# Self products of eight batches moved to the load of adj, with the schedule's ranks set anew, in a two-layer graph network on one core

## The chip, the cores and the metric

One core of one Trainium2 chip runs the whole program. The metric is device time in microseconds, the median of several runs. TensorE is PE in the profile, VectorE is DVE, ScalarE is ACT, GpSimd is POOL and SyncE is SP. SP only issues DMAs here.

## The reference, cut to what matters

Sixteen batches `x` of 1024 nodes by 128 features share one 0/1 matrix `adj`. Layer 0 is a graph attention, layer 1 a gated update that is repeated five times; each layer ends in a residual and a norm.

```python
# layer 0
h   = x @ others_weight
att = softmax(where(adj > 0, leaky_relu(u1[idx1] + u2[idx2]), -9e15), axis=1)
x   = layernorm(x + att @ h + x @ self_weight)
# layer 1, five steps: av = [adj @ h, adj @ h]
u3  = h @ u3_w.T
z   = sigmoid(av @ w3_w.T + u3);  r = sigmoid(av @ w4_w.T + u3)
hv  = tanh(av @ w5_w.T + (r * h) @ u5_w.T)
h   = (1 - z) * h + z * hv
out = layernorm(x + h)
```

(The biases are left out here.) The change is about `x + x @ self_weight`, which the kernel makes as one product of `x` with `self_w + identity`.

## The kernel before, in words

Everything lies transposed, features on the 128 partitions and nodes along the free side, in two halves of 512. `adj` stays in SBUF as `adj`, and four sums of its quarters as `tab`.

**Layer 0** (`layer0(b)`, for each batch b). The batch is loaded into a tile `xt` (two buffers). Eight small products `ps_g_ph` (L602) make `h`, which ACT copies to `hx`. Softmax weights follow on DVE and ACT. Scaled blocks `blk` (each as a high and a low part, by `hi_` on ACT and `lo_` on DVE) are multiplied with `adj` into `ps_acc_po` (L573). The self product x times `wsi` (`self_w` plus identity) is made by two matmuls for each batch: L858 into its own PSUM bank `ps_acc_px` for the left half, which DVE adds at L865, and L872 at the start of the accumulation of `ps_acc_po` for the right half, whose sum ACT copies out at L884. Then come a transpose, the norm (`layernorm`: DVE statistics, POOL power, ACT scale) and a transpose back into the state `hT`.

**Layer 1** works on pairs of batches (q = b // 2). `messages(q, s, k)` multiplies the states of a pair with `adj` in step s, by a scheme with seven products from `adj` and `tab` (banks `ps_acc_a`, `gz`, `ps_acc_c`), or plainly (`ps_acc`) for the (pair, step) in `PLAIN`. `gates(b, s, soon)` then does for each half: L1103 (u3 times h), ACT copy to `gz`, L1113 twice (gates r and z), tanh on ACT, r times h on DVE, L1129 and L1130 (candidate), tanh on ACT, three DVE operations that update `hT`. `leave(b, s)` turns the new state for the next step: a 32x32 transpose on DVE (L531), four DMAs to DRAM (`away`), one back (`back`, tile `G`), and a split into high and low parts (L561 on ACT, L565 on DVE). For the (pair, step) in `TURNED` it uses four TensorE transposes (L523) instead. After the last step `o` tiles (two buffers) take the first layer's result from DRAM (L1197), DVE adds (L1205), a norm follows, and L1216 stores the output.

**The order of the work** is not that of the code. Each operation is given to `Plan` with an engine, a length, a rank and what it reads and writes. `Plan.order()` plays these through on an own clock: an engine that is free takes the ready operation with the lowest rank whose buffers can be had. The program is emitted in that order, and each engine runs its list strictly in that order. DVE and ACT lengths are multiplied by `MARGIN`. The dictionary `D` holds rank offsets by kind of operation; `rank_of(b, s)` is 10 for each pair and 4.2 for each step, with `LATER` added for the last batch.

**Fillers.** `IDLE` operations of rank 9000, of two transposes of the identity each (L413), fill the places where, by the plan's clock, TensorE has nothing ready. All of them write one PSUM tile `("ps", "idle")`; it is one of the six buffers of kind `ps`, and by the plan it is held from the first filler to the last. `gz` has two more buffers.

The parts below are those that the change touches.

Of the kernel before, what the change touches and what calls it, by code (L numbers as in the profile page):

```python
# [9 lines left out]
F32 = mybir.dt.float32  # L10
# [3 lines left out]
ALU = mybir.AluOpType  # L14
AX = mybir.AxisListType

P = 128
N = 1024
HALF = 512
NC = N // P  # L20
STEPS = 5
# [4 lines left out]
LOW, HIGH = -20.0, 100.0  # L26
TINY = 1e-30
PLAIN = {(0, 0), (0, 1), (0, 2), (7, 2), (7, 3), (7, 4)}
LATER = 3
TURNED = {(7, 3)}  # L30
IDLE = 100


class Plan:
# [4 lines left out]

    MARGIN = 1.15
    SAME = {"PE": 0, "DVE": 60, "ACT": 60, "POOL": 60, "SP": 2500, "DMA": 0}
    LAG = {"PE": 250, "DVE": 150, "ACT": 170, "POOL": 200, "SP": 2500, "DMA": 2400}

# [87 lines left out]
def kernel(  # L133
# [51 lines left out]
    nc = tc.nc  # L185
    B = x_t.shape[0]
# [6 lines left out]
    wsi = const.tile([P, P], F32, tag="wsi", name="wsi")  # L193
# [19 lines left out]
    def exact(pools):  # L213

        def pool(name, bufs, space=None):
# [35 lines left out]
            "D": (6, [P, HALF], F32, bass.MemoryType.DRAM),  # L251
            "X": (24, [P, HALF + 16], F32, bass.MemoryType.DRAM),
            "yd": (24, [P, HALF], F32, bass.MemoryType.DRAM),
            "ud": (2, [3, N], F32, bass.MemoryType.DRAM),
            "ps": (6, [P, HALF], F32, PS),
            "gz": (2, [P, HALF], F32, PS),
# [39 lines left out]

        D = dict(m=-0.4, pu=1.4, u=0.4, pr=0.8, pz=1.4, r=-0.3, pv=0.2, z=0.3, hv=0.2, h=0.6, tr=1.0, o=3.6, ln=3.9)
        D.update(out=4.2, l1=-9, l2=-5, l3=-4, l4=-4, l5=-5, l6=-3.5, l7=-1, l8=0)

        def on_pe(b, what):  # L300

# [9 lines left out]
        def rank0(b):  # L311
            return 10 * (b // 2) - 1 * (1 - b % 2) + -1.0
# [6 lines left out]
        boot = ("hT", "boot")  # L319
# [99 lines left out]
        for k in range(kinds["gz"][0]):  # L419
            pe(F, -99, lambda k=k: fill_(k), reads=[(("ident",), 0)], writes=[(("gz", "fill", k), 0)])  # L420

        for i in range(IDLE):
            pe(2 * TR, 9000, idle_, reads=[(("ident",), 0)], writes=[(("ps", "idle"), 0)])

# [3 lines left out]
        def sums():  # L428
# [5 lines left out]
            nc.vector.tensor_tensor(bh, bias[:, 0:2], bias[:, 3:4].to_broadcast([P, 2]), ALU.add)  # L434
            nc.vector.tensor_scalar(bh, bh, 0.5, None, ALU.mult)

        def own_weights():
            pb_ = ("ps", "g", "b")
            pe(150, -4.6, lambda: column_(pb_, slice(2 * P, 3 * P), 5), reads=[(ws, "b"), (("rz", 0), 1)], writes=[(pb_, 0)])
            dve(160, -4.3, lambda: nc.vector.tensor_copy(bias, T(pb_)[:, 0:5]), reads=[(pb_, 0)], writes=[(("bias",), 0)])  # L440
            dve(270, -4.5, self_, reads=[(boot, "ws"), (("ident",), 0), (("zs", 0), NC - 1)], writes=[(("wsi",), 0)])
            dve(1000, -4.2, sums, reads=[(boot, "late"), (("bias",), 0), (("uw",), 0), (("rz", 0), 1)], writes=[(("wm",), 0)])

        def adj_tables(c):
# [16 lines left out]
        def quarter(i, j):  # L461
            return lambda c: adj[:, 4 * i + c, j * HALF : (j + 1) * HALF]
# [107 lines left out]
        def product(bank, blk, right, first, last, cs=range(4), seeded=False):  # L570
            terms = [(k, c) for c in cs for k in range(2)]
            for i, (k, c) in enumerate(terms):
                nc.tensor.matmul(  # L573
                    T(bank),
                    T(blk)[:, k, c, :],
                    right(c),
                    start=(first and i == 0),
                    stop=(last and i == len(terms) - 1),
                    skip_group_check=seeded,
                )  # L580


        def layer0(b):
# [266 lines left out]
            def add_():  # L850
                nc.vector.tensor_tensor(T(yT[0]), T(yT[0]), T(yT[1]), ALU.add)

            dve(V, rank, add_, reads=[(yT[0], "p"), (yT[1], "p")], writes=[(yT[0], "s")])
            px = ("ps", "acc", b, "px")
            pe(
                F,
                rank,
                lambda: nc.tensor.matmul(T(px), wsi, T(xt)[:, left], start=True, stop=True),  # L858
                reads=[(xt, 0), (("wsi",), 0), (yT[1], "p")],
                writes=[(px, 0)],  # L860
            )
            dve(
                V,
                rank,
                lambda: nc.vector.tensor_tensor(T(yT[0]), T(px), T(yT[0]), ALU.add),  # L865
                reads=[(px, 0), (yT[0], "s")],
                writes=[(yT[0], 0)],
            )
# [3 lines left out]
                nc.tensor.matmul(T(po2), wsi, T(xt)[:, right], start=True, stop=False)  # L872

            begun = [(hl[1][0], c, 1) for c in range(4)]
            pe(F, rank, px2_, reads=[(xt, 1), (("wsi",), 0), *begun], writes=[(po2, 0)])
            for g in range(2):
                pe(
                    8 * R,
                    rank,
                    lambda g=g: product(po2, hl[1][g], quarter(g, 1), False, g == 1),  # L880
                    reads=[(k, 4 * g + c, j) for k, j in ((hl[1][g], 0), (hl[1][g], 1), (("A",), 1)) for c in range(4)],
                    writes=[(po2, 0)],
                )
            act(A, rank, lambda: nc.scalar.copy(T(yT[1]), T(po2)), reads=[(po2, 0), (yT[0], "s")], writes=[(yT[1], 0)])  # L884

            for g in range(2):
                rank = rank0(b) + D["l5"]
# [271 lines left out]
        def leave(b, s):  # L1159

            rank = rank_of(b, s)
            hT = ("hT", b)
            for g in range(2):

                def h(g=g):
                    return T(hT)[:, g * HALF : (g + 1) * HALF]

                k, d = ("T", b, s, g), ("X", b, s + 1, g)
                if s < STEPS - 1 and on_pe(b, s):
                    t = ("ps", "t", b, s, g)  # L1170
# [23 lines left out]
                sp(  # L1194
                    450,
                    rank + D["o"],
                    lambda o=o, yd=yd: nc.sync.dma_start(T(o).rearrange("p c d -> p (c d)"), T(yd)),  # L1197
                    reads=[(yd, 0), (hT, g)],
                    writes=[(o, "y")],
                )  # L1200

                def last(t=t, o=o, flat=on_pe(b, s)):
                    x = T(o).rearrange("p c (a j) -> p c a j", a=4)
                    n = T(t).rearrange("p (c a j) -> p c a j", c=4, a=4) if flat else chunks(T(t))
                    nc.vector.tensor_tensor(x, n, x, ALU.add)  # L1205
# [55 lines left out]
        def sum_flags():  # L1261
            nc.tensor.matmul(T(("ps", "t", "flag"))[0:1, 0:2], T(("rstd", "ends"))[:, 0, 3:4], ones, start=True, stop=True)

        for c in range(NC):
            adj_tables(c)
        for c in range(NC // 2):
# [4 lines left out]
        for k, (q, s) in enumerate(sorted(pairs, key=lambda x: rank_of(2 * x[0], x[1]))):  # L1271
            soon = messages(q, s, k)
            for b in (2 * q, 2 * q + 1):
                gates(b, s, soon)
                leave(b, s)
        for i in range(2 * NC):
            look_at(i)
        late = rank_of(B, 0) - 2
# [280 lines left out]
```

## Time and profile before

| what | value |
|---|---|
| median of 3 runs | 1466.42 us (1464.65 to 1471.49) |
| profiled execution | 1466.58 us, of which the span is 1464.7 us |
| granted TensorE clock, mean | 0.994 |
| PE busy | 1442.1 us (98%), 5052 matmul records |
| DVE busy | 1168.4 us (80%) |
| ACT busy | 898.9 us (61%) |
| POOL busy | 152.9 us (10%) |
| DMA | 174.21 MB, 119 GB/s over the span |
| fillers L413 | 200 matmul records, 4.9 to 49.4 us |
| L858 and L872, the self products | 16 matmuls each (32 records each) |

A 128x512 product of full fp32 shows as two records, a product with `adj` (in `float32r`) and a 128x128 transpose as one. Records of neighbouring matmuls overlap in time, so what one costs is read from start to start, not from its duration. Busy time counts the overlap once. "Idle before" is the time for which an engine stood still ahead of an instruction, with what released it.

### The profile page before, as it was taken

The page shows a single profiled execution, that of the slowest core. Times are in us where ns is not written, and L with a number is a line of the kernel's source. Part 1 is how long each engine was busy: PE and PEld are TensorE (multiplying, and loading weights), DVE is VectorE, ACT ScalarE, POOL GpSimd, SP SyncE. Part 2 cuts the span into 40 slices and gives each one's busy share as a digit, 9 for nine tenths or more (in the row PEclk, how much of TensorE's full clock was granted, in tenths as well). Part 3 has the DMA queues.
Part 4 walks back from the last instruction along what each step waited for, and adds up shares of the span by engine and source line. Part 5 has one row for each costly group of instructions (what it writes and reads, how often), then busy time and mean ns, then how long its engine had stood idle before and what let it go on. Part 6 is the DMA issues. An engine that isn't in the chain of part 4 may idle for free.

```text
span 1464.7 us, 17943 instructions
## 1 busy us (share of the span) xinstructions
PE 1442.1 (98%) x5052; PEld 904.6 (62%) x5052; DVE 1168.4 (80%) x2757; ACT 898.9 (61%) x1792; POOL 152.9 (10%) x265
## 2 busy tenths in 40 slices
PE   9999899999999999999999999999999999999995
PEld 7766665666666666665566656665666665665563
DVE  6887788888888788888888888887888877757444
ACT  5456565676657666576756676566674666555544
POOL 0201000011002020110201120011110202000102
PEclk9999999999999999999999999999999999999998
DMA  4145534654335542464433643355433464223301
GB/s 164 58 126 162 167 78 117 172 177 128 87 100 151 173 131 65 121 172 140 117 98 117 187 123 94 108 161 155 116 85 96 134 184 114 58 72 87 91 24 45
DMA packets 208384, 174.21 MB, mean 119 GB/s; under 512 B 34879, under 2 KB 158486, under 8 KB 208278
## 3 DMA queue, kind: packets, MB, share of 16 engines
q1 hardware_dynamic: 207714, 172.15, 41.1%
q10 hardware_dynamic: 564, 0.85, 0.2%
q8 instruction: 41, 0.67, 0.2%
q14 instruction: 65, 0.53, 0.1%
HBM read 94.63 MB, written 78.29 MB: 118 GB/s over the span
## 4 chain that ended last, share of the span: by engine, by line
PE 94%; DVE 2%; DMA 1%; ACT 1%; POOL 1%; issue 0%; SPq 0%; POOLq 0%; DVEq 0%
PE ps_acc_a L573 17%; PE ps_g_r L1113 9%; PE ps_g_v L1129 9%; PE ps_g_v L1130 9%; PE gz L1113 9%; PE ps_g_r L1103 9%; PE ps_acc_c L573 8%; PE ps_acc_po L573 8%; PE ps_acc L573 6%; PE gz L573 4%; PE ps_g_ph L602 2%; PE ps_idle L413 1%; PE ps_acc_po L872 1%; PE ps_acc_px L858 1%; ACT o L510 1%; DMA blk_boot<-in_adj_dram 0%
## 5 line engine op out<-in xcount | busy, mean ns | idle before, releaser
L1129 PE MATMUL ps_g_v<-m,wm 128*128 128x512 f32 x320 | 163.4, 592 | 0.0
L1130 PE MATMUL ps_g_v<-r,u5h 128*128 128x512 f32 x320 | 163.3, 592 | 0.0
L1140 DVE TENSOR_TENSOR hv<-hv,hT 128x512 f32<-128x512 f32 x160 | 109.7, 687 | 63.2 <-ACT hv L1133 62.8
L1113 PE MATMUL ps_g_r<-m,wm 128*128 128x512 f32 x320 | 158.8, 594 | 1.1 <-ACT gz L1106 1.1
L1113 PE MATMUL gz<-m,wm 128*128 128x512 f32 x320 | 157.7, 592 | 0.0
L1103 PE MATMUL ps_g_r<-hT,u 128*128 128x512 f32 x320 | 152.7, 592 | 0.0
L1123 DVE SCALAR_TENSOR_TENSOR r<-r,hT 128x512 f32<-128x512 f32 x160 | 109.1, 686 | 50.9 <-ACT r L1116 50.1
L573 PE MATMUL ps_acc_a<-tab,blk_s 128*128 128x512 f32 x544 | 146.7, 411 | 0.4 <-ACT m L1056 0.4
L573 PE MATMUL ps_acc_po<-adj,blk 128*128 128x512 f32 x512 | 144.5, 428 | 0.0
L1116 ACT ACTIVATE r<-ps_g_r,bh 128x512 f32<-128x512 f32 x160 | 109.4, 686 | 46.8 <-PE ps_g_r L1113 46.5
L573 PEld LDWEIGHTS ps_acc_a<-tab,blk_s 128*128 128x128 f32 x544 | 100.4, 188 | 34.4 <-issue 6.7
L1116 ACT ACTIVATE z<-gz,bh 128x512 f32<-128x512 f32 x160 | 109.5, 688 | 19.1 <-PE gz L1113 18.8
L573 PEld LDWEIGHTS ps_acc_po<-adj,blk 128*128 128x128 f32 x512 | 96.0, 188 | 39.4 <-issue 14.6
L1154 DVE SCALAR_TENSOR_TENSOR hT<-hv,hT 128x512 f32<-128x512 f32 x160 | 107.9, 676 | 1.6
L1147 DVE SCALAR_TENSOR_TENSOR hv<-z,hv 128x512 f32<-128x512 f32 x160 | 108.1, 677 | 1.0 <-ACT z L1116 0.3
L1106 ACT COPY gz<-ps_g_r 128x512 f32<-128x512 f32 x160 | 91.5, 574 | 28.1 <-PE ps_g_r L1103 26.7
L531 DVE STREAM_TRANSPOSE T<-hT 128x512 f32<-128x512 f32 x150 | 104.9, 701 | 4.1 <-DMA X<-T 3.7
L1130 PEld LDWEIGHTS ps_g_v<-r,u5h 128*128 128x128 f32 x320 | 60.5, 189 | 76.8 <-issue 61.9
L1113 PEld LDWEIGHTS gz<-m,wm 128*128 128x128 f32 x320 | 60.5, 190 | 74.4 <-issue 74.0
L573 PE MATMUL ps_acc<-adj,blk_h 128*128 128x512 f32 x384 | 99.9, 416 | 3.9 <-DVE blk_h L565 3.9
L1133 ACT ACTIVATE hv<-ps_g_v,nb 128x512 f32<-128x512 f32 x80 | 54.9, 689 | 68.6 <-PE ps_g_v L1130 68.6
L1113 PEld LDWEIGHTS ps_g_r<-m,wm 128*128 128x128 f32 x320 | 59.4, 189 | 58.5 <-issue 44.6
(166 smaller groups left out, 2520.7 us busy)
## 6 DMA issues: line engine op xcount, KB each, us to landing
G<-X SPq DMA_DIRECT2D x152, 256.0 KB
X<-T SPq DMA_DIRECT2D x600, 64.0 KB
yd<-y SPq DMA_DIRECT2D x32, 256.0 KB
o<-yd SPq DMA_DIRECT2D x32, 256.0 KB
out_dram<-o SPq DMA_DIRECT2D x32, 256.0 KB
xt<-in_x_dram SPq DMA_DIRECT2D x15, 512.0 KB
pb<-ud SPq DMA_DIRECT2D x14, 512.0 KB
D_y<-T_y SPq DMA_DIRECT2D x112, 64.0 KB
```

What stands on the lines that cost most here:

```text
L531: nc.vector.transpose(T(t).rearrange("p (b c i) -> p b c i", b=4, c=4), turned(src()))
L573: nc.tensor.matmul(T(bank), T(blk)[:, k, c, :], right(c), start=(first and i == 0), stop=(last and i == len(terms) - 1), skip_group_check= ...
L1103: nc.tensor.matmul(T(pr), u3, h(), start=True, stop=True)
L1106: nc.scalar.copy(T(pz), T(pr))
L1113: nc.tensor.matmul(T(p_), wm[:, j, :], T(m), start=False, stop=True, skip_group_check=True)
L1116: nc.scalar.activation(T(t), T(p_), AF.Tanh, bias=bh[:, j : j + 1], scale=0.5 * sg)
L1123: lambda r=r, h=h: nc.vector.scalar_tensor_tensor(T(r), T(r), 1.0, h(), ALU.add, ALU.mult),
L1129: nc.tensor.matmul(T(pv), wm[:, 2, :], T(m), start=True, stop=False)
L1130: nc.tensor.matmul(T(pv), u5h, T(r), start=False, stop=True)
L1140: lambda hv=hv, h=h: nc.vector.tensor_tensor(T(hv), T(hv), h(), ALU.subtract),
L1147: lambda hv=hv, z=z: nc.vector.scalar_tensor_tensor(T(hv), T(z), 1.0, T(hv), ALU.add, ALU.mult),
L1154: lambda hv=hv, h=h: nc.vector.scalar_tensor_tensor(h(), T(hv), 0.5, h(), ALU.mult, ALU.add),
```

## The change

The self product of batches 4 to 11 (`AHEAD`) is made at the start of the program. Each of these batches is loaded once more, into tiles of kind `hT` that no state uses yet, two matmuls of rank 8000 (before the fillers) multiply it with `wsi`, ACT copies each half into a tile of kind `m`, and SP stores it to DRAM tensors `PX`. In `layer0` of these batches the two matmuls go; instead SP loads 512 KB from `PX` into a tile of kind `xt`, DVE adds the left half from SBUF, and the right half is added to `ps_acc_po` by DVE where ACT had copied. `wsi` is made earlier. `TURNED` gets (0, 0), so the four states of pair 0 after step 0 are turned on TensorE. There are 80 fillers of two transposes instead of 100. New fillers `hum` (60 of two transposes, PSUM tile of their own) can run once the last pair has its second to last messages. `MARGIN`, `LATER` and ten offsets in `D` have new values.

```diff
-LATER = 3
-TURNED = {(7, 3)}
-IDLE = 100
+LATER = 2.5
+AHEAD = range(4, 12)
+TURNED = {(0, 0), (7, 3)}
+IDLE = 80
+HUM = 60
...
-    MARGIN = 1.15
+    MARGIN = 1.1
...
+            "PX": (len(AHEAD), [P, N], F32, bass.MemoryType.DRAM),
...
-        D = dict(m=-0.4, pu=1.4, u=0.4, pr=0.8, pz=1.4, r=-0.3, pv=0.2, z=0.3, hv=0.2, h=0.6, tr=1.0, o=3.6, ln=3.9)
-        D.update(out=4.2, l1=-9, l2=-5, l3=-4, l4=-4, l5=-5, l6=-3.5, l7=-1, l8=0)
+        D = dict(m=-0.4, pu=1.4, u=0.2, pr=0.6, pz=1.4, r=1.7, pv=0.2, z=0.3, hv=0.2, h=0.6, tr=1.2, o=4.0, ln=3.3)
+        D.update(out=4.0, l1=-9, l2=-3, l3=-3, l4=-4, l5=-5, l6=-3.5, l7=0, l8=0)
...
+        def hum_():
+            for j in range(2):
+                nc.tensor.transpose(T(("ps", "hum"))[:, j * P : (j + 1) * P], ident, ident)
+
+        def hum():
+            for i in range(HUM):
+                pe(2 * TR, 9000, hum_, reads=[(("m", B - 1, STEPS - 2, 1), 0)], writes=[(("ps", "hum"), 0)])
...
+        def ahead():
+            dve(270, -8, self_, reads=[(boot, "ws"), (("ident",), 0)], writes=[(("wsi",), 0)])
+            for b in AHEAD:
+                x, d = ("hT", "x", b), ("PX", b)
+                sp(450, -90, lambda x=x, b=b: nc.sync.dma_start(T(x), x_t[b]), writes=[(x, "sent")], lag=0)
+                plan.add("DMA", 8 * 190, -102, lambda: None, reads=[(x, "sent")], writes=[(x, 0)])
+                for e in range(2):
+                    bank, px = ("ps", "ahead", b, e), ("m", "px", b, e)
+                    hs = slice(e * HALF, (e + 1) * HALF)
+
+                    def px_(bank=bank, x=x, hs=hs):
+                        nc.tensor.matmul(T(bank), wsi, T(x)[:, hs], start=True, stop=True)
+
+                    pe(F, 8000, px_, reads=[(x, 0), (("wsi",), 0)], writes=[(bank, 0)])
+                    act(A, -5.5, lambda bank=bank, px=px: nc.scalar.copy(T(px), T(bank)), reads=[(bank, 0)], writes=[(px, 0)])
+                    sp(
+                        450,
+                        -20,
+                        lambda d=d, px=px, hs=hs: nc.sync.dma_start(T(d)[:, hs], T(px)),
+                        reads=[(px, 0)],
+                        writes=[(d, e)],
+                    )
...
-            dve(270, -4.5, self_, reads=[(boot, "ws"), (("ident",), 0), (("zs", 0), NC - 1)], writes=[(("wsi",), 0)])
...
+            px = ("xt", b, "px") if b in AHEAD else ("ps", "acc", b, "px")
+            if b in AHEAD:
+                d = ("PX", b)
+                sp(
+                    450,
+                    rank0(b) + D["l3"],
+                    lambda d=d: nc.sync.dma_start(T(px), T(d)),
+                    reads=[(d, 0), (d, 1), (hx, 3)],
+                    writes=[(px, 0)],
+                    lag=2800,
+                )
+            else:
+                pe(
...
-                lambda: nc.vector.tensor_tensor(T(yT[0]), T(px), T(yT[0]), ALU.add),
+                lambda: nc.vector.tensor_tensor(T(yT[0]), T(px)[:, left], T(yT[0]), ALU.add),
...
-            pe(F, rank, px2_, reads=[(xt, 1), (("wsi",), 0), *begun], writes=[(po2, 0)])
+            if b not in AHEAD:
+                pe(F, rank, px2_, reads=[(xt, 1), (("wsi",), 0), *begun], writes=[(po2, 0)])
...
-                    lambda g=g: product(po2, hl[1][g], quarter(g, 1), False, g == 1),
+                    lambda g=g: product(po2, hl[1][g], quarter(g, 1), b in AHEAD and g == 0, g == 1),
...
-            act(A, rank, lambda: nc.scalar.copy(T(yT[1]), T(po2)), reads=[(po2, 0), (yT[0], "s")], writes=[(yT[1], 0)])
+            if b in AHEAD:
+                dve(
+                    V,
+                    rank,
+                    lambda: nc.vector.tensor_tensor(T(yT[1]), T(po2), T(px)[:, right], ALU.add),
+                    reads=[(po2, 0), (px, 0), (yT[0], "s")],
+                    writes=[(yT[1], 0)],
+                )
+            else:
+                act(A, rank, lambda: nc.scalar.copy(T(yT[1]), T(po2)), reads=[(po2, 0), (yT[0], "s")], writes=[(yT[1], 0)])
...
+        ahead()
         for c in range(NC):
             adj_tables(c)
...
+        hum()
         for i in range(2 * NC):
             look_at(i)
```

More of the change, by code (lines that the diff above doesn't have):

```diff
@@ L853, in layer0 @@
             dve(V, rank, add_, reads=[(yT[0], "p"), (yT[1], "p")], writes=[(yT[0], "s")])
[L854 to L861, printed above, removed]
+            px = ("xt", b, "px") if b in AHEAD else ("ps", "acc", b, "px")
[11 more added lines that the diff above has]
+                pe(
+                    F,
+                    rank,
+                    lambda: nc.tensor.matmul(T(px), wsi, T(xt)[:, left], start=True, stop=True),
+                    reads=[(xt, 0), (("wsi",), 0), (yT[1], "p")],
+                    writes=[(px, 0)],
+                )
             dve(
@@ L883, in layer0 @@
                 )
-            act(A, rank, lambda: nc.scalar.copy(T(yT[1]), T(po2)), reads=[(po2, 0), (yT[0], "s")], writes=[(yT[1], 0)])
+            if b in AHEAD:
+                dve(
+                    V,
+                    rank,
+                    lambda: nc.vector.tensor_tensor(T(yT[1]), T(po2), T(px)[:, right], ALU.add),
+                    reads=[(po2, 0), (px, 0), (yT[0], "s")],
+                    writes=[(yT[1], 0)],
+                )
+            else:
+                act(A, rank, lambda: nc.scalar.copy(T(yT[1]), T(po2)), reads=[(po2, 0), (yT[0], "s")], writes=[(yT[1], 0)])
             for g in range(2):
```

## The prediction

> **What bounds the kernel now.** I read the page's busy line, then the chain, then TensorE's own waits.
>
> ```profile
> PE 1442.1 (98%) x5052; PEld 904.6 (62%) x5052; DVE 1168.4 (80%) x2757; ACT 898.9 (61%) x1792; POOL 152.9 (10%) x265
> ...
> PE 94%; DVE 2%; DMA 1%; ACT 1%; POOL 1%; issue 0%; SPq 0%; POOLq 0%; DVEq 0%
> ```
>
> ```profile
> PE ps_acc L573 <- DVE blk_h L565: 3.9, 1, 3.9
> PE ps_t L523 <- DVE hT L1154: 2.8, 2, 2.4
> PE gz_fill L417 <- POOL ones L383: 1.3, 1, 1.3
> PE ps_g_r L1113 <- ACT gz L1106: 1.1, 2, 0.7
> PE ps_p L679 <- DVE T_ws L398: 1.0, 1, 1.0
> PE ps_acc_a L573 <- ACT m L1056: 0.4, 1, 0.4
> ```
>
> These six rows are all of TensorE's waits (us, times, longest): 10.5 us of 1464.7. So time is TensorE's list of work, plus those waits, plus a tail after its last instruction. That makes the fillers work too. The chain, in order of time, runs through them (start, length):
>
> ```profile
> 13.29 4.37 PE ps_idle L413 x40
> ...
> 22.78 5.46 PE ps_idle L413 x50
> ...
> 123.95 3.72 PE ps_acc_po L573 x16
> ```
>
> A filler transpose costs 5.46 / 50 = 0.109 us, a product with adj 3.72 / 16 = 0.2325 us. The TensorE timeline gives the self product (two records, L858 to L872 from start to start 0.86 us) and the one long wait:
>
> ```profile
> 36.57 1.02 PE L858 MATMUL ps_acc_px<-xt,wsi 128*128 128x512 f32 x2
> 37.43 1.02 PE L872 MATMUL ps_acc_po<-xt,wsi 128*128 128x512 f32 x2
> ...
> 153.23 10.24 PE L573 MATMUL ps_acc<-adj,blk_h 128*128 128x512 f32 x31 [3.88 <-DVE blk_h L565]
> ```
>
> After that wait 31 products took 10.24 us; at 0.2325 they are 7.2. The table of windows says why (next to last but one column is the granted clock):
>
> ```profile
> 154.00:156.00 2.00, 2.00 (x7) 1.52 (x6) 1.85 (x10) 0.43 (x2) 0.00 (x0) 0.50 0.79 222
> ```
>
> So this one place costs 3.9 + 3.0 = 6.9 us. Last, the tail, from the timeline of all engines:
>
> ```profile
> 1447.49 1.64 ACT L510 ACTIVATE o<-o,rstd_o 128x128 f32<-128x128 f32 x4
> 1447.56 1.02 PE L1130 MATMUL ps_g_v<-r,u5h 128*128 128x512 f32 x2
> ...
> 1449.59 2.32 SPq L1197 DMA_DIRECT2D o<-yd x2
> ...
> 1454.32 0.66 DVE L1205 TENSOR_TENSOR o<-ps_t,o 128x512 f32<-128x512 f32 x1
> ```
>
> The last candidate product ends at 1447.56 + 0.86 = 1448.42 (call it V); from V to the end of the span are 16.3 us. The second L1197 issue waits for the store of an `o` buffer that ACT L510 filled.
>
> **What the Trainium skill says.** "TensorE: Matmul & The Clock Gate", section "What's actually happening": an idle window of about 3.4 us halves the clock. The trace agrees: after 3.88 us it was 0.50. The same page, "Part 4: PE-mode transpose", says that transposes don't bring the full clock; here the trace disagrees: 50 fillers in a row ran at 0.109 us with the clock at 1.00, so I cost `hum` at 0.109. "Perfetto Trace Analysis", section "Tensor Engine Instruction (MATMUL, LD_WEIGHTS)", calls ACT, DVE and GpSimd strict FIFO. The trace agrees at the wait: L565 had its data split by ACT at 147.5 to 148.1, yet ran at 152.53, behind eight operations of batch 1 and one of batch 3.
>
> **The change, part by part.** The order in which the changed program's instructions stand shows where things go; durations are those above.
>
> 1. *Self products.* Sixteen leave the steady part and sixteen enter the start: 13.8 - 13.8 = 0. They save only if they replace fillers. The order has, ahead of the first step's products, 116 filler transposes and 16 self products (12.6 + 13.8 = 26.4 us) where there were 200 transposes (21.8): the start gets 4.6 us longer. In that sense the change does less than its name says: the fillers are mostly joined, not replaced.
> 2. *Fillers.* Of the 160 left, 154 stand ahead of V: 46 fewer, -5.0 us. Of these, 12 stand soon after the start, 26 among the last 330 rows.
> 3. *TURNED.* 16 more transposes: +1.7 us. Off DVE go four L531 (0.70 each), off SP 16 stores and four loads.
> 4. *The long wait.* In the new order, L565's counterpart for batch 0 stands ahead of batch 1's whole update, and z of batch 0's left half comes earlier. The other half's split stands behind seven DVE operations (some 0.65 each) of batch 1: I work it out as ready 0 to 0.7 us late. So -6.9 + 0.5 = -6.4.
> 5. *Last gate.* Batch 15's last L1113 moves behind V: -0.9.
> 6. *ACT at the start.* Sixteen copies (0.57 each, row of L1106) stand in its list, among them before the scaling of the first norm. That was ready at 46.7 before; TensorE comes to the transposes that need it at about 46: +1.0 with one more small wait. The five first x loads issue after the small loads, which end at 19.7 us; 512 KB at the 388 GB/s of that stretch is 1.3 us, and a 256 KB o<-yd load took 2.9 from issue to landing: the first lands at about 23.3 and each next one 1.3 later, against a first use at 24.3, the second batch's at 26.0 and the third's at 34. DVE's bias copy and ACT's scaling queue behind these.
> 7. *Added DVE and DMA work.* Eight adds (0.69) replace eight ACT copies; DVE is at 80%, the steady wait is nil: 0. DMA gets 12 MB (eight times 0.5, three times) on 174. The eight loads from `PX` may be issued once `hx` is done; TensorE has 50 us or more of other work in the list between those two points, so they land in time: 0. What stands behind one of them on SP, such as a G load for the next step, could be late; bounds 0 to +3, I take 0.
> 8. *Ranks and MARGIN.* Not shown by any row. As a test I added up TensorE's work between the r gate and the L1130 that needs it: median 4.4 us before, 5.4 after, least 2.6 and 3.0; before, no L1130 ever waited. Least work between L1103 and its L1113 is 0.7 and 1.1. So the new order is not tighter. Bounds -1 (the waits of L1113) to +15 (the rival below); I take +0.5.
> 9. *Tail.* In the new order ACT scales o of batch 14 after batch 15's last z: V + 1.7, ends V + 3.4; 2.4 us to the next SP issue (from 1449.13 to about 1451.5 before), 2.7 to landing, V + 8.4; from L1205 to the end were 10.4, less 0.5 of queueing on POOL: V + 18.3 against V + 16.3, +2.0. The 100 last `hum` transposes end at about V + 15.5, covered.
>
> Sum: -5.0 + 1.7 - 6.4 - 0.9 + 1.0 + 0.5 + 2.0 = -7.1. The profiled execution took 1466.58 (median 1466.42, so it stands for the runs): 1459.5 us, -0.5%. About 0.5%, 7.3 us, is what a measurement of this kernel tells from no change; the sum lies at that edge.
>
> **Rivals.** *The fillers were free.* If TensorE must wait where 46 transposes went, -5.0 is lost: 1464.5. For it: DVE is busy 9.55 of 10 us from 20 to 30 us, so the start may be DVE's. Against it: no TensorE wait from 10 to 149 us, and self products take the places.
>
> *Slower: PSUM buffers.* The filler tile was given back at 49 us; now fillers stand as late as row 1310, so one of six `ps` buffers is held to the end and the steady part turns on five. Where ACT or DVE is late, TensorE then waits for a buffer. One stall as at 149 us costs 6.9; it takes 14.4 us (7.3 + 7.1) to end slower, two such stalls and a little. Three give 1459.5 + 20.7 = 1480. For it: MARGIN is smaller, and L1123 got rank 1.7. Against it: DVE operations start 0.61 us apart where V x 1.1 allows 0.67, and the plan itself put no filler between rows 165 and 963, so it saw no such wait.
>
> *Hum ends the span.* If the clock halves in the tail, 100 transposes take 21.8 us instead of 10.9: V + 26, 1467. Against it: TensorE has no gap there.
>
> **How the numbers follow.** The sum holds: 0.63, of it 0.38 below 1459.1 and 0.25 above (its own range 1455 to 1464). Fillers free: 0.14, nearly all within 0.5%. PSUM stalls: 0.17, slower. Hum or a longer tail: 0.06, mostly within. Faster 0.40, same 0.43, slower 0.17. The range goes from 1453 to 1473: it leaves out most of the stalls and a few hundredths below.
>
> **What would show it.** Right: TensorE's wait on L565 gone or under 1 us and no window at 0.50 around 155 us; the first `ps_acc` product at about 55 us instead of 49.5; V near 1439; 18 us from V to the end. Wrong: new rows in TensorE's waits in the steady part, over 3 us in sum, or a wait for `ps_ahead` at 24 us.

## The result, and the profile after

The changed kernel took 1479.78 us (median of six runs, 1477.91 to 1486.99) against 1467.68 us for the kernel before in runs beside it: a ratio of 1.0091, 95% interval 1.0073 to 1.0109. It is slower by 0.9%, where 1459.5 us and a range of 1453 to 1473 were forecast. The profiled execution is the longest of the six (1486.99 us, span 1485.2): in it TensorE's clock was halved in four places; the run that kept the full clock throughout took 1477.91.

The page's busy line and chain (section 1 and 4):

```profile
PE 1460.4 (98%) x5148; PEld 915.9 (62%) x5148; DVE 1167.5 (79%) x2761; ACT 900.1 (61%) x1800; POOL 189.7 (13%) x265
...
PE 71%; DVE 8%; DMA 7%; POOL 5%; ACT 4%; issue 2%; SPq 2%; DVEq 0%; POOLq 0%; ACTq 0%
```

DVE and ACT do as much as before. GpSimd (POOL) has the same 265 instructions and is busy 189.7 us instead of 152.9: in the mean each takes longer. The chain, 94% TensorE before, leaves TensorE for DVE, DMA, GpSimd and ACT: something else now ends waits. TensorE's own waits (total, times, longest) say which engine releases it:

```profile
PE ps_g_r L1169 <- ACT gz L1162: 8.7, 7, 2.7
PE ps_acc_a L608 <- ACT m L1112: 5.3, 5, 2.2
PE gz L608 <- ACT gz L1112: 2.7, 1, 2.7
PE gz_fill L420 <- POOL ones L386: 1.3, 1, 1.3
PE ps_g_v L1186 <- DVE r L1179: 0.7, 1, 0.7
```

(L608, L1169, L1162 and L1112 are L573, L1113, L1106 and L1056 of before.) Before, waits for ACT's copies `gz` and `m` were 1.5 us in all; now they are 16.7. The long wait on `blk_h` is gone, as forecast: 0.23 us of it are left at 173.27. In its place stand stalls spread over the steady part, of which the longest but one is shown second:

```profile
173.27 5.63 PE L608 MATMUL ps_acc<-adj,blk_h 128*128 128x512 f32 x23 [0.23 <-DVE blk_h L600]
...
481.94 3.45 PE L608 MATMUL gz<-adj,blk_x 128*128 128x512 f32 x8 [2.67 <-ACT gz L1112]
```

The eight products after the stall take 3.45 us instead of 1.86. The table of windows has the granted clock (next to last but one column) at 0.50 there:

```profile
482.00:484.00 2.00, 2.00 (x5) 1.61 (x6) 1.97 (x6) 0.71 (x2) 1.07 (x3) 0.50 0.68 200
```

The tail, from the timeline of all engines:

```profile
1468.83 0.39 SPq L1272 DMA_DIRECT2D out_dram<-o  x1
...
1472.26 0.32 SPq L1253 DMA_DIRECT2D o<-yd  x1
...
1474.92 0.69 DVE L1261 TENSOR_TENSOR o<-ps_t,o 128x512 f32<-128x512 f32 x1 [4.58 <-DMA o<-yd]
```

The last candidate product ends at 1464.97, so V to the end of the span is 20.2 us (16.3 before, 18.3 forecast).

The following table cuts V of a profiled execution into the waits after 55 us (all idle times of TensorE's timeline of 0.16 us and more), the time lost to a halved clock (busy time times one less the granted clock, from windows of 2 us), and the rest, which is work with the waits of the start. It holds some of the experiments told below. The row of the changed kernel is that of its longest run, 7.2 us above its median, so its waits and half clock are more than those of a usual run.

| kernel | V | waits after 55 us | half clock | rest | V to end |
|---|---|---|---|---|---|
| before | 1448.4 | 5.4 | 3.0 | 1440.0 | 16.3 |
| changed | 1465.0 | 18.4 | 6.5 | 1440.1 | 20.2 |
| e5, no wait for GpSimd | 1441.4 | 5.2 | 0.0 | 1436.2 | 19.0 |
| e18, one input on DVE | 1442.7 | 5.3 | 0.0 | 1437.4 | 20.2 |
| e13, light power and tail | 1442.2 | 4.7 | 0.0 | 1437.5 | 19.0 |
| e14, the same on before | 1447.2 | 5.2 | 2.8 | 1439.2 | 16.0 |

Of the 20.4 us between the profiled executions of the changed kernel and the kernel before, 13.0 are waits, 3.5 half clock, 0.1 the rest, and 3.9 the tail.

A stall costs more than its recorded idle time: between the changed kernel and e5, whose lists are the same, V differs by 23.6 us, of which 13.2 are waits and 6.5 half clock; 3.9 are left. About 0.2 us of that go with each of the 11 stalls that the changed kernel has more (18 against 7): the product at 379.80 starts 2.40 us later against e5 than the one ahead of it, with a recorded wait of 2.22. The other half of the 3.9 is open.

### The profile page after: what moved, and what is told of

Its sections match the earlier page's. It is cut to its first block, busy times and chain, and to the rows that moved or that the text cites. A ratio compares the mean times of both kernels' runs of the same rounds, so it can differ in the third digit from the quotient of the medians.

```text
span 1485.2 us, 18097 instructions
## 1 busy us (share of the span) xinstructions
PE 1460.4 (98%) x5148; PEld 915.9 (62%) x5148; DVE 1167.5 (79%) x2761; ACT 900.1 (61%) x1800; POOL 189.7 (13%) x265
## 4 chain that ended last, share of the span: by engine, by line
PE 71%; DVE 8%; DMA 7%; POOL 5%; ACT 4%; issue 2%; SPq 2%; DVEq 0%; POOLq 0%; ACTq 0%
PE ps_acc_a L608 12%; PE ps_g_r L1169 7%; PE ps_g_v L1186 7%; PE gz L1169 7%; PE ps_g_v L1185 7%; PE ps_g_r L1159 7%; PE ps_acc_c L608 7%; PE ps_acc_po L608 5%; PE ps_acc L608 4%; PE gz L608 3%; DMA G<-X 3%; SPq L576 2%; POOL rstd_y L533 2%; ACT y L545 1%; PE ps_idle L416 1%
## 5 line engine op out<-in xcount | busy, mean ns | idle before, releaser
L1169 PE MATMUL ps_g_r<-m,wm 128*128 128x512 f32 x320 | 161.3, 603 | 8.7 <-ACT gz L1162 8.7
L1169 PE MATMUL gz<-m,wm 128*128 128x512 f32 x320 | 159.4, 595 | 0.0
L608 PE MATMUL ps_acc_a<-tab,blk_s 128*128 128x512 f32 x544 | 147.0, 412 | 5.4 <-ACT m L1112 5.3
L608 PE MATMUL ps_acc_po<-adj,blk 128*128 128x512 f32 x512 | 140.2, 420 | 0.0
L608 PEld LDWEIGHTS ps_acc_a<-tab,blk_s 128*128 128x128 f32 x544 | 101.3, 188 | 39.8 <-ACT m L1112 8.6
L1179 DVE SCALAR_TENSOR_TENSOR r<-r,hT 128x512 f32<-128x512 f32 x160 | 108.6, 684 | 20.7 <-ACT r L1172 20.5
L533 POOL TENSOR_SCALAR rstd_y<-mv_y 128x4 f32<-128x4 f32 x32 | 30.5, 954 | 738.5 <-DVE mv_y L529 671.6
L608 PEld LDWEIGHTS ps_acc_po<-adj,blk 128*128 128x128 f32 x512 | 95.9, 188 | 35.5 <-issue 10.8
L1162 ACT COPY gz<-ps_g_r 128x512 f32<-128x512 f32 x160 | 91.3, 573 | 32.0 <-PE ps_g_r L1159 29.7
L1210 DVE SCALAR_TENSOR_TENSOR hT<-hv,hT 128x512 f32<-128x512 f32 x160 | 108.8, 680 | 1.8
L1203 DVE SCALAR_TENSOR_TENSOR hv<-z,hv 128x512 f32<-128x512 f32 x160 | 108.8, 680 | 1.0
L1169 PEld LDWEIGHTS gz<-m,wm 128*128 128x128 f32 x320 | 60.7, 191 | 72.8 <-issue 72.1
L608 PE MATMUL ps_acc<-adj,blk_h 128*128 128x512 f32 x384 | 102.9, 418 | 0.2 <-DVE blk_h L600 0.2
L1169 PEld LDWEIGHTS ps_g_r<-m,wm 128*128 128x128 f32 x320 | 59.7, 191 | 65.1 <-issue 37.9
```

The source lines that it names most:

```text
L608: nc.tensor.matmul(T(bank), T(blk)[:, k, c, :], right(c), start=(first and i == 0), stop=(last and i == len(terms) - 1), skip_group_check= ...
L1162: nc.scalar.copy(T(pz), T(pr))
L1169: nc.tensor.matmul(T(p_), wm[:, j, :], T(m), start=False, stop=True, skip_group_check=True)
L1179: lambda r=r, h=h: nc.vector.scalar_tensor_tensor(T(r), T(r), 1.0, h(), ALU.add, ALU.mult),
L1203: lambda hv=hv, z=z: nc.vector.scalar_tensor_tensor(T(hv), T(z), 1.0, T(hv), ALU.add, ALU.mult),
L1210: lambda hv=hv, h=h: nc.vector.scalar_tensor_tensor(h(), T(hv), 0.5, h(), ALU.mult, ALU.add),
```

## The experiments

Four theories stood before the first run. **R**: the new ranks and MARGIN put ACT's copies too late. **P**: the filler tile held to the end costs a PSUM buffer (the rival on record). **A**: the DMAs of AHEAD delay others. **S**: any other order deals the waits anew, and the order of before has few. Each group of experiments ran beside the kernel before, whose medians lay between 1466.2 and 1467.7 us; a difference of a microsecond between groups says nothing.

**One part at a time (e1 to e4).** In e1 the diff on the kernel before is:

```
-TURNED = {(7, 3)}
+TURNED = {(0, 0), (7, 3)}
```

> The kernel before with (0, 0) added to TURNED and nothing else: 16 more transposes (+1.7 us), four DVE transposes and a DRAM round trip less. In its order on DVE the blk_h operation of batch 0, third step, stands behind much the same list as before. Theory R (the new ranks and MARGIN let ACT's list be caught late): no new stalls, 1463 to 1469. Theory P (the filler tile held to the end costs a PSUM buffer): the fillers are all at the start as before, so the same, 1463 to 1469. Theory A (the loads and stores of AHEAD delay other DMAs): the same. Theory S (any change of the order redeals which of ACT's waits reach TensorE, worth up to some 15 us either way): TensorE's waits after 60 us are a new set, with a sum anywhere from 0 to 20 us, and the time anywhere from 1455 to 1480.

Measured: 1487.35 us, ratio 1.0144 (1.0115 to 1.0173). This one setting costs more than the whole change, and more than even S allowed (1480). The waits after 55 us are 16.2 us.

e2 gives the kernel before the new ranks, MARGIN and LATER only:

```
-    MARGIN = 1.15
+    MARGIN = 1.1
-LATER = 3
+LATER = 2.5
```

and the two lines of D from the changed kernel.

> The kernel before with the new D, MARGIN and LATER, without AHEAD, TURNED, IDLE and HUM. R: the stalls come with it: TensorE waits over 10 us in the steady part with several half-clock stretches, 1472 to 1482. P: all 200 fillers stand at the start, six ps buffers remain, waits under 3 us: 1457 to 1462 (the long wait of before is gone). A: no AHEAD, so no new stalls: 1457 to 1462. S: a set of its own, 1455 to 1480.

Measured: 1478.85 us, 1.0099 (1.0076 to 1.0122); waits 15.4 us.

e3 is the opposite: the changed kernel with the three old settings.

> The changed kernel with the old D, MARGIN and LATER. R: the new stalls go, 1458 to 1466. P: the filler tile is still held to the end (120 of 280 filler and hum transposes stand behind row 1200), so the stalls stay: 1474 to 1485. A: the 24 DMAs of AHEAD stay and so do the stalls: 1474 to 1485. S: a set of its own, 1455 to 1485.

Measured: 1505.43 us, 1.0280 (1.0257 to 1.0304); waits 32.6 us. R expected a gain here and falls: with the other parts in, the new ranks save 26 us against the old ones. S's range (to 1485) is exceeded too. A falls as the only cause of stalls: e1 and e2 have no AHEAD and have them.

e4 frees the filler tile early in the changed kernel:

```
-IDLE = 80
+IDLE = 56
```

> The changed kernel with IDLE at 56 instead of 80: all 112 fillers left stand ahead of the first products, so the filler tile is given back at the start and the steady part has six ps buffers in the plan; 42 fewer transposes ahead of the end of the last candidate product (-4.6 us). P: the stalls in the steady part fall under 3 us, and with them the half clock: 1479.8 - 4.6 - 17 = about 1458. R and A: the stalls stay: about 1475. S: the order changes, so a set of its own: 1460 to 1485.

Measured: 1478.06 us, 1.0095 (1.0073 to 1.0118); waits 16.1 us, of which 0.4 (`ps_g_ph` for ACT's `r`) can be for a free buffer. P falls: the rival's 1480 us was met by another mechanism.

**The same instructions in another order (e8).** On the kernel before:

```
-    MARGIN = 1.15
+    MARGIN = 1.14
```

> The kernel before with MARGIN 1.14 instead of 1.15, that is the same instructions with the same ranks, of which some 500 of 2809 on TensorE change places. S (the order of before is one of few without stalls; any other of the same make has 15 to 25 us of them): TensorE's waits after 55 us 10 to 25 us, 1472 to 1490. Rival R2 (what hurts are the parts themselves, the larger ranks, TURNED and the new DMAs, each by itself): 1464 to 1468, waits under 7 us.

Measured: 1494.93 us, 1.0195 (1.0174 to 1.0216): a change of one percent in MARGIN, the factor of DVE's and ACT's lengths in the plan, costs 28 us. TensorE's three longest rows of waits in e8:

```profile
PE ps_acc_a L573 <- ACT m L1056: 8.5, 4, 3.6
PE ps_g_r L1113 <- ACT gz L1106: 5.0, 5, 2.7
PE ps_g_ph L602 <- DMA xt<-in_x_dram: 4.3, 1, 4.3
```

Of its 24.5 us of waits after 55 us, 13.9 are again for ACT's `m` and `gz`. The others are not: 4.3 are for a load of `xt`, and 3.8 for the split `blk_h`, a wait that the kernel before has as well (3.9). S is what is left so far: five new orders (e1 to e4, e8), each with 15 to 33 us of waits. It is a weak theory, though: it names no place, three of the five ran above its own range, and in e1, e3 and e4 the longest wait is for `blk_h` (3.6, 6.4 and 3.6 us). The longest wait of e8 for a copy, 3.6 us at 1080.88, is read back on ACT's own timeline, where each instruction starts only when the one ahead of it is through:

```profile
1073.02 0.57 ACT L1056 COPY m<-gz 128x512 f32<-128x512 f32 x1
1079.72 0.62 ACT L561 CAST blk_x<-G 128x512 fp32r<-128x512 f32 x1 [6.13 <-DMA G<-X]
1080.25 0.58 ACT L1056 COPY m<-ps_acc_a 128x512 f32<-128x512 f32 x1
```

The copy TensorE needs was next in the list behind a cast that stood 6.13 us for a load of G. Every stall of over 1 us for a copy of ACT in the changed kernel reads so: ahead of the copy stands a scaling that waits for a power on GpSimd (at 380, 482 and 1190 us) or a cast or copy that waits for a G or F load (169, 188, 944 and 1024). That is mechanism **M** for the changed kernel; its rival **X** says that ACT would be late anyhow.

**Taking M's waits away, every instruction in its place (e5 to e7).** In e5:

```
-    r = T(rstd)
+    r = mhalf
```

with bias and scale of the norm's scaling on ACT both taken from `r`.

> The changed kernel, every instruction in the same place on every engine; only the norms' scalings on ACT read the constant mhalf instead of rstd, so that they wait for no power on GpSimd (the norm is thereby left out of the result). Theory S with its mechanism M (a wait ahead of the gz or m copy in ACT's list reaches TensorE; of the stalls of the changed kernel those at 380, 482 and 1190 us, 6.8 us and 3.1 us of half clock, go back to a late power): these three go, the others stay: 1479.8 - 9.9 = 1470, between 1467 and 1474. Rival X (ACT's place in the list is late anyhow, the wait for GpSimd only stands ahead of another): within 3 us of 1479.8.

Measured: 1462.13 us, 0.9970 (0.9958 to 0.9981): 17.7 us less than the changed kernel, where 9.9 were expected. X falls.

```profile
PE ps_g_r L1169 <- ACT gz L1162: 3.7, 5, 1.5
PE gz_fill L420 <- POOL ones L386: 1.3, 1, 1.3
```

The waits for `m` are gone, and those for `gz` fell from 11.4 to 3.7 us. The difference to the 9.9 is in part in stalls put down to DMA: at 1024 us 2.69 became 0.46, at 944 us 1.19 became 0.23. For the one at 1024 the traces show how a power comes into it. In the changed kernel a power's first operation takes 2.91 us at 999.84, the scaling on ACT waits 2.02 us for that norm (at 1004.50), and DVE's transpose waits 2.31 us for the scaling (at 1006.19; 0.94 in e5). The stores and loads that ACT's casts then wait for come behind that transpose. So what a wait "goes back to" was the last of several delays.

e6 takes the wait for the store away from the loads of G and F:

```
-    lambda: nc.sync.dma_start(T(t), T(d)[:, 0:HALF]),
+    lambda: nc.sync.dma_start(T(t), x_t[0][:, 0:HALF]),
```

> The changed kernel, every instruction in the same place; only the loads of G and F read the first batch's input instead of X and D, so that they wait for no store (their data are thereby not the turned state). M: the stalls at 169, 188, 944 and 1024 us, 7.4 us and 3.4 us of half clock, go; those at 380, 482 and 1190 stay: about 1469, between 1465 and 1474. X: within 3 us of 1479.8. Should SP be what holds the rest up, its waits for stores end with it too and more than these four go: down to 1462.

Measured: 1481.05 us, 1.0100 (1.0084 to 1.0117): nothing gained. M's second half was wrong in its cause: G isn't late for its store. The four stalls that were to go are still there (1.1 to 1.7 us), while of the three that were to stay the one at 482 us shrank to 0.43 and the one at 1190 is gone. SP's timeline of e6, ahead of the stall at 189 us, shows the load behind four small loads in SP's list, and its own issue long:

```profile
174.21 3.60 SPq L701 DMA_DIRECT2D uu<-ud  x4
177.90 2.48 SPq L584 DMA_DIRECT2D G<-in_x_dram  x1
```

The load was through its issue at 180.38, and ACT's cast started at 182.91. That SP's list is what makes G late is read from this place, not tried.

e7 is both edits.

> Both of the last two together: no wait of ACT on GpSimd's power, none of a load on a store; all instructions in the same places (norm left out, turned state not used). M: 1479.8 - 9.9 - 10.8 = 1459, TensorE's waits after 55 us at most 5 us in sum where the changed kernel had 18.4, no stretch of half clock between 60 and 1440 us. X: waits over 12 us stay, 1473 to 1480.

Measured: 1467.55 us, 1.0006 (0.9998 to 1.0014). With e5's edit in, e6's made it 5.4 us slower. Why loads that need not wait cost time is open; they all read one place of the input, which may have its own price.

**Do the other orders pay for GpSimd too (e9, e10).** e5's edit on the kernel before and on e8:

> The kernel before with the norms' scalings on ACT reading the constant mhalf instead of rstd (norm left out), all instructions in the same places. M with S (the order of before is one in which the waits for GpSimd fall where TensorE has cover): of its 5.4 us of waits after 55 us none goes back to a power, so 1464 to 1467, within 0.3% of before. If instead the power costs every order about the same, as in the changed kernel (17.7 us): about 1450.

Measured: 1462.48 us, 0.9964 (0.9951 to 0.9977), 4.4 us less than before, and below the 1464 that was expected. V hardly moves (1447.6); 2.4 us are the tail (13.9 instead of 16.3), in which the last norm waits for no power.

> The kernel before with MARGIN 1.14 and the same scalings without a wait for GpSimd (norm left out). M: of its stalls those at 727 and 1403 us and perhaps 152 stand behind a norm, about 9 us with the half clock; the others stand behind G loads: 1494.9 - 9 = about 1486, between 1475 and 1490. If it is as in the changed kernel, where more went than the stalls traced to it: down to 1470. X (the norm only stands ahead of another wait): over 1491.

Measured: 1482.41 us, 1.0103 (1.0082 to 1.0124), 12.5 less than e8. So the price of the powers depends on the order: 4.4 us before, 12.5 in e8, 17.7 in the changed kernel. ACT's own waits for a power stand in the same sequence: 19.6, 29.2 and 55.6 us in all, of which 7 to 9 are in the tail. Without them the changed kernel (1462.13) and the kernel before (1462.48) take the same time.

**Why a power is slow (e11, e18).** The timeline of DVE, GpSimd and ACT in the changed kernel ahead of the stall at 380 us:

```profile
373.11 4.49 POOL L537 TENSOR_TENSOR rstd_o<-rstd_o 128x4 f32<-128x4 f32 x1
373.23 0.67 DVE L792 SCALAR_TENSOR_TENSOR junk<-adj,pb 128x512 f32<-128x512 f32 x1
...
373.83 0.67 DVE L1196 TENSOR_TENSOR hv<-hv,hT 128x512 f32<-128x512 f32 x1
...
375.65 0.67 DVE L600 TENSOR_TENSOR blk_x<-G,blk_x 128x512 fp32r<-128x512 f32 x1
376.26 0.68 DVE L1210 SCALAR_TENSOR_TENSOR hT<-hv,hT 128x512 f32<-128x512 f32 x1
...
377.47 0.69 DVE L566 STREAM_TRANSPOSE T<-hT 128x512 f32<-128x512 f32 x1
377.63 1.65 ACT L545 ACTIVATE o<-o,rstd_o 128x128 f32<-128x128 f32 x4 [3.13 <-POOL rstd_o L537]
```

A multiplication of 128x4 elements, which takes 0.20 us at 1472.52, takes 4.49 us here while DVE runs seven operations with two SBUF inputs back to back (between some of them only the 0.07 us read of an accumulator), and ends as DVE comes to a transpose, which has one. The Trainium skill, "SBUF — State Buffer", section "SBUF: two separate sides", has the cause: DVE and GpSimd share a port pair, and a DVE operation with two SBUF inputs holds it for the whole instruction against a GpSimd operation that reads SBUF. The trace agrees, and adds that GpSimd didn't get in between seven such instructions.

e11 leaves GpSimd two operations for a norm instead of four (three where the sign is negative). Nothing is left out of the result:

```
+    nc.vector.tensor_scalar(T(mv)[:, :, 1], T(mv)[:, :, 1], EPS, None, ALU.add)
+    if sg > 0:
+        nc.vector.tensor_scalar(T(mv)[:, :, 0], T(mv)[:, :, 0], -1.0, None, ALU.mult)
...
-    nc.gpsimd.tensor_scalar(r[:, 0, :], var, EPS, None, ALU.add)
-    nc.gpsimd.tensor_tensor(r[:, 0, :], r[:, 0, :], mhalf[:, 0:4], ALU.pow)
+    nc.gpsimd.tensor_tensor(r[:, 0, :], var, mhalf[:, 0:4], ALU.pow)
     if sg > 0:
-        nc.gpsimd.tensor_scalar(r[:, 1, :], mean, -1.0, None, ALU.mult)
-        nc.gpsimd.tensor_tensor(r[:, 1, :], r[:, 1, :], r[:, 0, :], ALU.mult)
+        nc.gpsimd.tensor_tensor(r[:, 1, :], T(mv)[:, :, 0], r[:, 0, :], ALU.mult)
```

> The changed kernel with the whole result: the addition of EPS and the change of sign of the mean move from GpSimd to DVE (behind the statistics), so that GpSimd has two small operations for a norm instead of four (three where the sign is negative); the plan and the order are as they were. M: half the time in which DVE can hold a power up, about half of the 17.7 us that the waits cost: 1471, between 1466 and 1476. If one held up operation is enough for a stall, 1475 to 1480.

Measured: 1466.60 us, 0.9999 (0.9991 to 1.0007): 13.2 us less than the changed kernel, at the low end of what was expected, for 96 operations moved from one engine to another.

e18 keeps GpSimd's four operations and changes DVE's:

```
-    nc.vector.tensor_tensor(T(hv), T(hv), h(), ALU.subtract)
+    nc.vector.transpose(T(hv), h())
```

and so for L1179, L1203 and L1210.

> The changed kernel, every instruction in the same place with the same waits; only the four DVE operations of a gate (r times h, and the three of the update) are 32x32 transposes of one of their two inputs instead of operations with two SBUF inputs (the update is thereby left out of the result). Theory H (DVE operations with two SBUF inputs hold GpSimd's small ones up): a power's first operation falls from 0.95 us in the mean to under 0.5, the stalls at 380, 482 and 1190 go, TensorE's waits after 55 us at most 8 us: 1462 to 1468. Rival (GpSimd is slow for another reason, its own sequencer or a wait for DVE's statistics): means and stalls as in the changed kernel, 1476 to 1481.

Measured: 1464.83 us, 0.9991 (0.9982 to 1.0000), where the rival expected 1476 or more. The same multiplication in the same place:

```profile
368.51 0.92 POOL L537 TENSOR_TENSOR rstd_o<-rstd_o 128x4 f32<-128x4 f32 x1
368.69 0.67 DVE L792 SCALAR_TENSOR_TENSOR junk<-adj,pb 128x512 f32<-128x512 f32 x1
...
369.30 0.69 DVE L1196 STREAM_TRANSPOSE hv<-hT 128x512 f32<-128x512 f32 x1
```

It is held for one DVE operation and through when the transpose comes. The powers' first operation, as a group, in the changed kernel and then in e18 (busy, mean ns):

```profile
L533 POOL TENSOR_SCALAR rstd_y<-mv_y 128x4 f32<-128x4 f32 x32 | 30.5, 954 | 738.5 <-DVE mv_y L529 671.6 <-ACT z L1172 51.5 <-ACT gz L1162 7.1
```

```profile
L533 POOL TENSOR_SCALAR rstd_y<-mv_y 128x4 f32<-128x4 f32 x32 | 11.3, 355 | 756.6 <-DVE mv_y L529 590.2 <-ACT z L1172 92.9 <-ACT gz L1162 40.6
```

Theory H is shown: the held-up powers are DVE's doing. ACT's waits for a power fall from 55.6 to 16.8 us in all.

**Due times nearer to the trace (e12, e15).** In the changed kernel:

```
-    plan.add("POOL", 2200, rank, power, reads=[(mv, 0)], writes=[(rstd, 0)])
+    plan.add("POOL", 4500, rank, power, reads=[(mv, 0)], writes=[(rstd, 0)])
-    lag=2300,
+    lag=4500,
```

where the lag is that of `back`, the loads of G and F.

> The changed kernel with two due times of the plan set nearer to what the trace shows: a power 4500 ns instead of 2200, a load of G or F landing 4500 ns after its issue instead of 2300. A new order, with the scalings and splits later in ACT's list. M: waits of ACT for GpSimd and for G fall to half, TensorE's waits after 55 us to under 9 us: 1460 to 1470. S alone (any new order is a new draw, whatever the due times say): 15 to 25 us of waits, 1475 to 1490.

Measured: 1471.82 us, 1.0031 (1.0021 to 1.0041), between the two theories; waits 9.6 us.

e15 adds the light power and the tail's edit of e13.

> The due times of e12 with the light power and the last o tiles from y0. If the two do the same work (keep ACT's list from standing behind a power): e12's one stall behind a norm goes (1.7 us and some half clock) and the tail's 3 us: 1471.8 - 6 = 1466. If due times add to it (the splits of G come later too): waits after 55 us under 5 us, 1460 to 1463.

Measured: 1470.07 us, 1.0030 (1.0018 to 1.0043); waits 9.8 us. That is above both expectations. The due times don't add to the light power; this order has long waits at 164 to 183 us that are not GpSimd's.

**The tail, and what the change is worth (e13, e14, e17, e16).** e13 is e11 with

```
-    o, yd = ("o", b, g), ("yd", b, g)
+    o, yd = ("y0" if b == B - 1 else "o", b, g, "o"), ("yd", b, g)
```

> The changed kernel with the light power and, beside it, the two o tiles of the last batch taken from the kind y0, which is free by then, so that the last loads of yd need not wait for the store of batch 14's o (all places in TensorE's list unchanged, result whole). If the tail's excess is that reuse: the wait of 4.6 us on L1264's counterpart goes, the end comes at V + 17 instead of V + 20.7, so 1466.6 - 3.5 = 1463, between 1461 and 1465. If the tail is set by something else (the stores on SP): 1466 to 1467.

Measured: 1464.34 us, 0.9986 (0.9977 to 0.9995), 2.3 less than e11. It is the only whole version here, with e17, that is below the kernel before by its interval, by 0.14%. The add's wait for `yd` fell from 4.6 to 2.6 us, but the end came at V + 19.0, not V + 17. The timeline shows what else ends late:

```profile
1446.81 11.08 PE L428 MATMUL ps_hum<-ident 128*128 128x128 f32 x100
...
1453.99 1.65 ACT L548 ACTIVATE y_o<-y_o,rstd_o 128x128 f32<-128x128 f32 x4 [3.03 <-POOL rstd_o L538]
```

`hum` ends at 1457.89, 2.3 us after the last scaling. In the eight runs without `hum` (the kernel before, e1, e2, e8 to e10, e14 and e16) the span ends 4.2 to 5.1 us after the last scaling; here it is 5.6, and in e5, where `hum` ends 4.1 us after the scaling, 7.5. In both the span ends 3.3 us after `hum`, at V + 19.0. So by the traces `hum` sets the end of e13 and of e5.

> The kernel before with the same two edits (light power, last o tiles from y0). M with S: no stall of before goes back to a power, so only its tail gets shorter, by at most the 0.7 us wait of its add on o<-yd and 0.5 us of a shorter last power: 1465, between 1463 and 1467. What the change is worth with a light power is then e13 less this one: near -2 us; by the sum on record, with the tail's +2.0 left out, it would be -9.

Measured: 1465.09 us, 0.9993 (0.9984 to 1.0002). e13 is 0.75 us below it, less than can be told.

e17 puts the last two `yd` loads ahead of the stores on SP:

```
-    reads=[(yd, 0), (hT, g)],
+    reads=[(yd, 0), (hT, g) if b < B - 1 else (("after",), b, s, g)],
```

> e13 with the last two loads of yd (batch 15) depending on the u product of their half instead of the finished hT, so that they stand on SP ahead of the stores of batch 14's o (TensorE's places unchanged up to the last candidate product; result whole). If the tail's excess is that place: the add's wait of 2.6 us for y_o<-yd goes, the end comes at V + 16.5 instead of V + 19.0: 1464.3 - 2.5 = 1462, between 1460.5 and 1463. If the stores or the norms set the end: 1464 to 1465.

Measured: 1465.17 us, 0.9988 (0.9980 to 0.9995): no gain over e13. The add no longer waits and the last scaling ends at 1457.39, yet the span ends at 1465.5. TensorE's timeline has the reason:

```profile
1451.56 0.60 PE L561 MATMUL ps_t<-ident,hT 128*128 128x128 f32 x4
1452.00 10.42 PE L428 MATMUL ps_hum<-ident 128*128 128x128 f32 x94
```

94 `hum` transposes end at about 1462.4, later than the last store was issued, and the span ends 3.1 us after them: `hum` sets the end here too. That is read from the traces; a smaller HUM wasn't tried.

e16 is e1 with the light power.

> The kernel before with (0, 0) in TURNED, as in e1, and the light power. Of e1's stalls of over 1 us one stands behind a power (1391 us, 2.6 us and about 1.5 of half clock), four behind G loads and one behind a transposed store: M by those roots 1487.4 - 4 = 1483, between 1480 and 1485. If the powers count beyond the stalls that are traced to them, as in the changed kernel: 1470 to 1478. If they count for nothing there: over 1486.

Measured: 1480.10 us, 1.0092 (1.0076 to 1.0109), 7.3 less than e1. The larger part of e1's loss stays; of its four waits over 1 us two stand behind G loads (ACT waited 4.0 and 4.6 us for them), one behind a power that ACT waited 2.4 us for.

## Why the prediction was wrong

*Step 8, ranks and MARGIN, failed.* It took +0.5 us for the new order. The waits after 55 us grew by 13.0 us and the half clock by 3.5, though the long wait was taken out; taking ACT's wait for GpSimd's powers away gave back 17.7 us (e5). The test in it was the wrong one: it added up TensorE's work between a gate and the product that needs it. That is cover on TensorE alone. The stalls come from what stands ahead of the `gz` or `m` copy in ACT's strict list, which no cover of TensorE shows. The prediction had the fact at hand (strict FIFO, L565 behind nine operations of DVE) and used it for the wait that goes, not for those that come. The upper bound of +15 in the same step was near the 16.5 us; but it was put to PSUM, at a chance of 0.17.

*The rival on PSUM buffers* had the side and even the size (1480 us), but by luck, since the mechanism was another: e4 gave the buffer back and kept 16 us of waits.

*Steps 1 to 3, 5 and 6 held.* Their sum with the start's +1.0 is -3.2 us; the rest of e5, in the same places without the stalls, is 1436.2 against 1440.0 before, -3.8. The first `ps_acc` product stands at 54.02 us (about 55 forecast), no load of AHEAD was waited for.

*Step 4 held for its wait* (3.88 to 0.23 us, no half clock near it), but not as a gain of the sum: in e13, e5 and e18, where GpSimd is out of the way, the waits after 55 us are again 4.7 to 5.3 us, in other places. What was gained is the 3 us of half clock.

*Step 7 (DVE's adds, the DMAs) at 0:* DVE's busy time is as before, and e1 and e2 have stalls without the added DMAs. What share the 24 added DMAs have in ACT's longer waits for G isn't separated.

*Step 9, the tail,* was mis-sized: +2.0 forecast, +3.9 measured. The scaling ended at V + 3.8 (3.4 forecast), but from the store's issue (1468.83) to the next `yd` load's (1472.26) are 3.4 us, where 2.4 were taken for the whole step from scaling to load. `hum` was just covered in the changed kernel (it ends at 1480.62, the last scaling at 1480.59). It set the end in e5, e13 and e17, where the rest of the tail was shorter. So the rival *hum ends the span* has a true core, without the halved clock that it rested on: 100 transposes at 0.109 us are enough to put the end at V + 19.0.

*What the change is worth* once neither kernel is held up by GpSimd: nothing that can be told (1464.34 against 1465.09 us; 1462.13 against 1462.48 without the powers' wait). V is 5.0 us earlier in e13 than in e14, and the tail 3.0 longer. Part of that tail is `hum`, which the change brought: from the last scaling to the end are 5.6 us in e13 against 4.4 in e14, and 7.5 in e5 against 5.1 in e9. An estimate from these: with a `hum` that ends in time, the change would be worth 2 to 3 us. No run shows it.

Open: why the order of before has so few stalls in its steady part. Its powers are 387 ns in the first operation's mean, as in e8 with 392 ns, so less hold-up of that operation isn't the whole of it; where a late copy falls against TensorE's list is the other part, and no run separates that.

## What to carry to other kernels

Where an engine works through one list in order, price a new order by what stands ahead of each copy that the bound engine needs, and by how late the entries there can be (a load of 5 us, a held-up GpSimd operation of 4.5), not by the cover on the bound engine. Before crediting a change with a time, run its order again with one of the plan's settings moved by a percent: here that alone was worth 28 us, more than TURNED (21) or the ranks (13) alone. Small GpSimd operations that others wait for belong away from runs of DVE operations with two SBUF inputs, or should be few: halving them gave back 13 us.

## What was not expected of the hardware

- A GpSimd operation of 0.2 us took 4.49 us beside seven DVE operations in a row with two SBUF inputs, and 0.92 us in the same place beside one.
- Pauses of TensorE well under the 3.4 us that the Trainium skill gives ("TensorE: Matmul & The Clock Gate", section "What's actually happening") were followed by a clock of 0.50: 1.92 us (at 1190), 2.00 (188), 2.67 (482) and 2.69 (1024). One of 2.22 us (380) was not, nor one of 2.25 in e6.
- The transposes of `hum`, 94 and 100 in a row, kept 0.109 us each, as the fillers did.
